# A third tile for the mixed rows, with its bytes taken from shared homes

## The chip, the cores and the metric

The kernel runs on one core of a Trainium2 chip. The metric is the device time of one execution in microseconds. The kernel before was run three times: 2610.47, 2618.05 and 2623.62 us, median 2618.05.

## The reference

Two residual layers act on x of shape (16, 16, 256, 256), batch and channel first. Cut to what is computed:

```python
def _L0_conv_ref(x, weight):          # 3x3 circular convolution, by way of FFTs
    ...
    return jnp.real(y).astype(x.dtype)

def _L1_conv_ref(x, ty, tx, weights_pole1, weights_pole2, weights_residue):
    alpha = jnp.fft.fft2(x, axes=(-2, -1))
    A = 1.0 / (omega1[:, None, None, None] - weights_pole1[None])
    Bm = 1.0 / (omega2[:, None, None, None] - weights_pole2[None])
    S = jnp.einsum('ikpq,oikp,xikq->oxik', weights_residue, A, Bm)
    output_residue1 = jnp.einsum('biox,oxik->bkox', alpha, S)
    C = jnp.einsum('biox,oikp->bikpx', alpha, A)
    D = jnp.einsum('bikpx,xikq->bikpq', C, Bm)
    output_residue2 = jnp.einsum('bikpq,ikpq->bkpq', D, weights_residue)
    x1 = jnp.fft.ifft2(output_residue1, s=(Ny, Nx), axes=(-2, -1)).real
    E1 = jnp.exp(weights_pole1[..., None] * tyc)
    E2 = jnp.exp(weights_pole2[..., None] * txc)
    F = jnp.einsum('kbpq,bipz->kbiqz', output_residue2, E1)
    x2 = jnp.einsum('kbiqz,biqx->kizx', F, E2).real
    return x1 + x2 / Nx / Ny

x = x + _L0_conv_ref(_gn(x), L0_conv_weight)
x = x + _L1_conv_ref(_gn(x), ...)
return x
```

`_gn` normalises groups of two channels. The second layer multiplies the spectrum of each image by a matrix S over channels that differs for every frequency (this is the mixing), transforms back, and adds a transient made of complex exponentials of the poles.

## The kernel before

The work runs in four stages, told apart in the trace by their matmuls.

1. From the start to about 565 us: the first layer's convolution (`ps_conv`, L305). Results go to DRAM (`vD`).
2. From 575 to 1194 us: the forward transforms. Spectra go to DRAM (`aD`), and the projections on the poles gather in `proj`.
3. Mixing, from about 1194 us: first `first_sums` and `finish_projections`, then, from 1219 to 1863 us, the loop that this text calls the mixing stage.
4. From 1860 us on: inverse transforms, the transient, and the output. It reads the mixed spectra `yD`, the exponentials `eD` and the projections `o2`.

**The mixing loop.** It goes over 32 groups g of frequencies, each in four steps n; a step is one pass of the loop body. In a step,

- `sums(n, ...)` makes with 16 small matmuls a part of the mixing matrices of the next group (`ps_s`, L1032), and `spread` brings them into the tile `sg`, half by ACT (L1049) and half by shuffles on DVE (L1052);
- `mix` makes four PSUM tiles `ps_mix` with 16 matmuls each (L1120), and each is copied into a quarter of the tile `yt` (L1233), two or three by ACT and the rest by DVE;
- `store` sends the filled `yt` to `yD` with four DMAs (L1134), and `load` fetches the spectra of the next group into `abd` (L1102 and L1107), four DMAs in the steps n = 1, 2, 3 and none in n = 0;
- in the first three steps of a group, `weights` prepares on DVE (`u`, `v`) and, in the third, on POOL (`w`, L930) the factors of a later group;
- `next(exps)` does one piece of the exponentials.

All these DMAs are issued by SP's queue in the order of the code. Each engine works off its own instructions in order, and that order is written out by hand (`manual_schedule`): what stands behind a waiting instruction on its engine waits too. `yt` comes from a pool of two buffers of 8 KB a partition, so the evictions of a step wait for the landing of the stores of two steps before.

**The exponentials** (`make_exps`) are generators whose pieces are put behind the steps. A pair of exponentials takes seven pieces: POOL multiplies the time axis by the imaginary parts (`s_th`, L1180), finds the number of turns (`s_rn`, L1181 to L1184) and subtracts them in three products (`s_tmp`, L1190, and L1191); POOL then adds the phase and clamps (L1194, L1195) while ACT makes the real exponentials (`s_ex`, L1198); two pieces later ACT takes the sine (L1201); then POOL multiplies the two (L1203) and folds the result into `s_ex` (L1205); and in the last piece SP stores `s_ex` to `eD` (L1210), with two DMAs for each of the first eight pairs and one for each of the other eight. Every tile of this pool has one buffer. The pieces are taken from the second group on, and the first four only load; between the eighth and the ninth pair lie four more pieces.

**Projections.** `first_sums` adds the two halves of `proj` into `accs` (L1062). `finish_projections` multiplies `accs` by the swap matrix `jmat` (four matmuls, L1090 and L1091) and copies the result to `o2` (L1092). In the kernel before, `proj`, `o2` and `jmat` have places of their own for the whole run, and `jmat` is loaded among the first constants (L158).

Two more things bear on the change. A tile called `between` of 1.5 KB only holds a place between two others. And pools of the mixing stage lie over places that the stage before has given up (`reuse_waits="tile"`): the first write to a tile waits for the last use of what lay there.

Of the kernel before, what the change touches and what calls it, by code (L numbers as in the profile page):

```python
# [9 lines left out]
FP = mybir.dt.float32  # L10
AF = mybir.ActivationFunctionType
ALU = mybir.AluOpType
# [4 lines left out]
B = 16  # L17
C = 16
N = 256
P = 128  # L20
PI = float(np.pi)
# [3 lines left out]
def conv_then_laplace_kernel(ctx: ExitStack, tc: tile.TileContext, a: dict, out: bass.AP):  # L25
# [15 lines left out]
    nc = tc.nc  # L41
    x = a["x"]

    cp = ctx.enter_context(tc.tile_pool(name="const", bufs=1))
# [9 lines left out]
    def const(name, shape):  # L54
        t = cp.tile(shape, FP, name=name, tag=name)
        later_loads.append((t, a[name]))
        return t
# [1 line left out]
    cols = const("cols", [P, 24])  # L59
    kmask = const("kmask", [P, C])  # L60
    fold2 = const("fold2", [P, 2, 64])
    o2 = cp.tile([P, B, 2, 16], FP, name="o2", tag="o2")
    proj = cp.tile([P, 2, B, 16, 2], FP, name="proj", tag="proj")
    jmat = cp.tile([P, 3, P], FP, name="jmat", tag="jmat")

    def pitched(name, rows, row, *split):

# [69 lines left out]
    def load_x(b, h):  # L137
        t = xp.tile([P, 18, N + 2], FP, name="xt", tag="xt")
        for i, j in zip(PARTS, PARTS[1:]):
            load_part(t, b, h, i, j)  # L140
        return t
# [13 lines left out]
    own = m16[:, 0:C:2]  # L155
    load_consts()
    halves[1] = [load_x(1, h) for h in range(2)]
    nc.sync.dma_start(out=jmat, in_=a["jmat"])  # L158
    ones = tp.tile([P, P], FP, name="ones", tag="ones")
    nc.vector.memset(ones, 1.0)  # L160
    tiny = wp.tile([P, 8], FP, name="tiny", tag="tiny")
# [557 lines left out]
    def pool(stage, name, bufs=1, **kw):  # L719
        return stage.enter_context(tc.tile_pool(name=name, bufs=bufs, reuse_waits="tile", **kw))  # L720
# [150 lines left out]
    p2 = ExitStack()  # L871
# [72 lines left out]
    for u in range(len(units) + 1):  # L944
# [27 lines left out]
        if last is not None:  # L972
            first_slots(b0, spec, *done)
            if b0 == B - 4:
                project(i, psd)
                (nc.sync if i + 1 < C else nc.scalar).dma_start(
                    out=aD[:, 2 * i : 2 * i + 2], in_=spec.rearrange("p r f b -> p r (f b)")
# [3 lines left out]
    ptab.close()  # L981


    yp = pool(p2, "yt", 2)
    g0 = pool(p2, "sg0")
    a0 = pool(p2, "abd0")
    wp = pool(p2, "w", 2)
    ep = pool(p2, "exps")
    up["u"] = pool(p2, "u")
    a1 = pool(p2, "abd2")  # L990
    zp = pool(p2, "between")
    tp = pool(p2, "ct")
    a2 = pool(p2, "abd3")
    g1 = pool(p2, "sg1")
# [10 lines left out]
        z.tile([P, 4, 4, 16, B], FP, name=f"abd{j}", tag=f"abd{j}") for j, z in ((2, a1), (3, a2))  # L1005
    ]

    zp.tile([P, 384], FP, name="between", tag="between")
    ct = tp.tile([P, 4, 8, N], FP, name="ct", tag="ct")
    nc.sync.dma_start(out=ct, in_=cD)  # L1010
    def next_step(steps, w):
# [42 lines left out]
    def first_sums():  # L1054

        nc.gpsimd.memset(pair, 0.0)
        wt, w128 = at_once(first_weights), at_once(weights(32))
        load(0, 1)  # L1060
        steps, w1 = weights(1), None
        nc.vector.tensor_tensor(accs, proj[:, :, :, :, 0], proj[:, :, :, :, 1], ALU.add)  # L1062
        sg = new_sg(0)
        other = up["u"].tile([P, 2, 2 * C], FP, name="other", tag="other")
        for h, w in enumerate((wt, w128)):
            for n in range(4):
                fy = slice(P * h, P * h + P)
                ps = sums(n, w)
                spread(
                    n,  # L1070
                    (sg[:, fy], [z[:, :, fy].rearrange("p q n -> p n q") for z in ps]),
                    (other[:, 1 - h], [z[:, :, P * (1 - h)] for z in ps]),
                )
                if 4 * h + n in (3, 4, 5):
                    w1 = next_step(steps, w1)
        for h in range(2):
            o, d = sg[:, P * h], other[:, h]
            nc.vector.tensor_tensor(d, d, o, ALU.subtract)
            nc.vector.scalar_tensor_tensor(o, d, fixrow, o, ALU.mult, ALU.add)
        for jq in range(2, 4):  # L1080
            nc.gpsimd.memset(abd[jq], 0.0)
            load(0, jq)
        return sg, w1

    def finish_projections():


        for ro in range(2):
            ps = pm.tile([P, B, 16], FP, name="ps_o", tag="ps_mix")
            nc.tensor.matmul(ps, lhsT=jmat[:, 0], rhs=accs[:, ro], start=True, stop=False)  # L1090
            nc.tensor.matmul(ps, lhsT=jmat[:, 2 - ro], rhs=accs[:, 1 - ro], start=False, stop=True)  # L1091
            nc.vector.tensor_copy(o2[:, :, ro], ps)  # L1092

    def load(g, jq, rows=range(4)):


        if jq == 0:
            return
        for s in rows:
            src = aD[4 * g + s].rearrange("r (c h n) -> r c h n", c=4, h=4)  # L1100
            if jq == 1:
                nc.sync.dma_start(  # L1102
                    out=pair[s::4, s].rearrange("r c h j b -> r c (h j b)"),
                    in_=src[:, :, 0:2].rearrange("r c h n -> r c (h n)"),
                )
            else:
                nc.sync.dma_start(  # L1107
                    out=abd[jq][s::4, s].rearrange("r c j b -> r c (j b)"), in_=src[:, :, jq]
                )
# [51 lines left out]
    def make_exps(which):  # L1161


        pl = ep.tile([P, C, 2], FP, name="s_pl", tag="s_pl")
        nc.sync.dma_start(out=pl, in_=a[f"pole_e{which + 1}"])
        t = ep.tile([P, N], FP, name="s_t", tag="s_t")
        nc.sync.dma_start(out=t, in_=a[("ty", "tx")[which]].to_broadcast([P, N]))
        sign, phase, turns = (cols[:, 2 + 3 * which + j : 3 + 3 * which + j] for j in range(3))
        pim = ep.tile([P, C], FP, name="s_pim", tag="s_pim")
        for _ in range(4):  # L1170
            yield
        nc.gpsimd.tensor_scalar(pim, pl[:, :, 1], sign, None, ALU.mult)
        for q in range(8):
            th = ep.tile([P, 2, N], FP, name="s_th", tag="s_th")
            rn = ep.tile([P, 2, N], FP, name="s_rn", tag="s_rn")
            tmp = ep.tile([P, 2, N], FP, name="s_tmp", tag="s_tmp")
            ex = ep.tile([P, 2, N], FP, name="s_ex", tag="s_ex")
            for j in range(2):
                i = 2 * q + j
                nc.gpsimd.tensor_scalar(th[:, j], t, pim[:, i : i + 1], None, ALU.mult)  # L1180
            nc.gpsimd.tensor_scalar(rn, th, 1.0 / (2 * PI), turns, ALU.mult, ALU.add)  # L1181
            magic = 1.5 * 2.0**23
            nc.gpsimd.tensor_scalar(rn, rn, magic, None, ALU.add)
            nc.gpsimd.tensor_scalar(rn, rn, magic, None, ALU.subtract)  # L1184
            yield
            c1 = 6.28125
            c2 = float(np.float32(1.93500518798828125e-3))
            c3 = 2 * np.pi - c1 - c2
            for c in (c1, c2, c3):
                nc.gpsimd.tensor_scalar(tmp, rn, float(c), None, ALU.mult)  # L1190
                nc.gpsimd.tensor_tensor(th, th, tmp, ALU.subtract)  # L1191
                if c == c2:
                    yield
            nc.gpsimd.tensor_scalar(th, th, phase, 3.1415925, ALU.add, ALU.min)  # L1194
            nc.gpsimd.tensor_scalar(th, th, -3.1415925, None, ALU.max)  # L1195
            for j in range(2):
                i = 2 * q + j
                nc.scalar.activation(ex[:, j], t, AF.Exp, scale=pl[:, i, 0:1])  # L1198
            yield True
            yield  # L1200
            nc.scalar.activation(th, th, AF.Sin)  # L1201
            yield True
            nc.gpsimd.tensor_tensor(th, th, ex, ALU.mult)  # L1203
            for op, eo in ((ALU.add, 0), (ALU.subtract, 1)):
                nc.gpsimd.tensor_tensor(  # L1205
                    ex[:, :, eo * P : eo * P + P], th[:, :, 0:P], th[:, :, N - 1 : P - 1 : -1], op
                )
            yield
            for o in range(2 - which):
                nc.sync.dma_start(  # L1210
                    out=eD[which][o, :, 2 * q : 2 * q + 2].rearrange("p i e t -> p i (e t)"),
                    in_=ex,
                )
            yield

    p2.enter_context(tc.manual_schedule())
    accs = yp.tile([P, 2, B, 16], FP, name="accs", tag="yt")
    ahead, wt = first_sums()
    finish_projections()
    unmix = None  # L1220
    exps, late = chain(make_exps(0), make_exps(1)), None
    for g in range(32):
        sg, w_now = ahead, wt
        steps = weights(g + 2) if g < 30 else iter(())
        ahead = new_sg(g + 1) if g < 31 else None
        for n in range(4):
            evict = sums(n, w_now) if ahead is not None else []
            yt = yp.tile([P, 2, 4 * B, 16], FP, name="yt", tag="yt")
# [27 lines left out]
    ep = pool(p3, "et")  # L1256
# [353 lines left out]
```

## Time and profile before

| | us |
|---|---|
| median of three runs | 2618.05 |
| the profiled execution's own time | 2623.94 |
| its span, first to last instruction | 2622.1 |
| mixing stage, within the span | 1219 to 1863 |
| PE busy in the mixing stage | 604.0 |
| POOL busy in the mixing stage | 389.2 |

The page's first lines give each engine's share of the span, and a strip of 40 slices shows it over time:

```profile
PE 2468.6 (94%) x35314; PEld 1885.3 (72%) x35314; DVE 1980.8 (76%) x3772; ACT 1432.6 (55%) x2599; POOL 1290.5 (49%) x1179
...
PE   5998999989999999998999999999799999999998
...
POOL 1333378433333333333666645766555565555553
```

A digit is the busy share of a slice of 65.6 us in tenths. [...] The mixing stage fills the slices 19 to 29. In rows of the trace, "SPq" is SP's queue, whose rows are DMA issues and not transfers; `<-` in a wait names the one that ended it. Where two shapes are given, the first is that of the output, as partitions by elements. A name such as L1134 is line 1134 of the kernel before.

### The profile page before, as it was taken

How to read it: one execution, taken by the hardware profiler on the slowest of the kernel's cores; microseconds unless marked ns; L12 is line 12 of the kernel's file. 1: busy time of each engine (PE TensorE's matmuls, PEld its weight loads, DVE VectorE, ACT ScalarE, POOL GpSimd, SP SyncE). 2: the span in 40 equal slices, each digit the busy share in tenths (PEclk: the TensorE clock that was granted, in tenths of full speed). 3: DMA queues.
4: the chain of work that ended last, by engine and by line, in shares of the span. 5: the costliest groups of instructions: out<-in, count | busy, mean ns of one | idle time of the engine just before them, and what ended most of it. 6: DMA issues, size and time to landing. Idle time of an engine off the chain costs nothing.

```text
span 2622.1 us, 84262 instructions
## 1 busy us (share of the span) xinstructions
PE 2468.6 (94%) x35314; PEld 1885.3 (72%) x35314; DVE 1980.8 (76%) x3772; ACT 1432.6 (55%) x2599; POOL 1290.5 (49%) x1179
## 2 busy tenths in 40 slices
PE   5998999989999999998999999999799999999998
PEld 2444455567777777775878778788688888888887
DVE  7777788848888888887877878887276676667666
ACT  2565566666666666665666656666244444444443
POOL 1333378433333333333666645766555565555553
PEclk9999999989999999999999999999899999999999
DMA  7888878854655655655777777777988888888884
GB/s 274 276 279 282 294 270 294 297 211 177 240 195 209 242 220 194 245 225 190 225 229 214 226 225 222 222 227 228 253 302 289 291 292 279 299 289 287 291 287 174
DMA packets 318011, 653.17 MB, mean 249 GB/s; under 512 B 49174, under 2 KB 163990, under 8 KB 305728
## 3 DMA queue, kind: packets, MB, share of 16 engines
q1 hardware_dynamic: 316464, 640.57, 72.4%
q8 instruction: 278, 4.55, 0.7%
q0 software_dynamic: 896, 3.02, 0.4%
q10 hardware_dynamic: 272, 4.19, 0.4%
q14 instruction: 101, 0.83, 0.1%
HBM read 368.15 MB, written 280.36 MB: 247 GB/s over the span
## 4 chain that ended last, share of the span: by engine, by line
PE 58%; DVE 7%; DMA 4%; SPq 3%; ACT 3%; POOL 2%; issue 1%; ACTq 0%; DVEq 0%; POOLq 0%
PE ps_mix L1120 9%; PE ps_y L777 9%; PE ps_y L785 8%; PE ps_p L1361 7%; PE ps_f L1385 7%; PE ps_f L1386 7%; PE ps_x L820 5%; DMA yD<-yt 4%; PE ps_s L1032 2%; SPq L1134 2%; PE ps_h L1345 2%; PE psd L805 1%; DVE r L1394 1%; DVE ol L1396 1%; DVE ol L1397 1%
## 5 line engine op out<-in xcount | busy, mean ns | idle before, releaser
L1120 PE MATMUL ps_mix<-abd,sg 128*64 128x128 f32 x8192 | 482.2, 276 | 39.4 <-DMA yD<-yt 16.6
L1120 PEld LDWEIGHTS ps_mix<-abd,sg 128*64 128x64 f32 x8192 | 451.9, 138 | 92.9 <-ACT yt L1233 55.7
L1325 POOL TENSOR_TENSOR u<-yk 128x512 f32<-128x512 f32 (+1 forms) x268 | 358.2, 1369 | 314.7 <-PE ps_p L1361 249.1
L305 PE MATMUL ps_conv<-xt,wc 32*32 32x512 f32 x12288 | 445.6, 602 | 36.0 <-issue 26.1
L305 PEld LDWEIGHTS ps_conv<-xt,wc 32*32 32x32 f32 x12288 | 251.1, 103 | 217.6 <-issue 127.0
L793 ACT ACTIVATE t<-ps_y,vmr 128x384 f32<-128x384 f32 x512 | 297.1, 580 | 161.1 <-PE ps_y L785 161.1
L1052 DVE STREAM_SHUFFLE sg<-ps_s 128x512 f32<-128x512 f32 (+1 forms) x264 | 329.1, 1316 | 0.0
L777 PE MATMUL ps_y<-tabE,vq 128*128 128x256 f32 x1024 | 313.2, 388 | 11.0 <-DVE vq L766 9.4
L785 PE MATMUL ps_y<-tabO,vq 128*128 128x256 f32 x1024 | 305.9, 380 | 0.0
L275 POOL TENSOR_TENSOR pair<-pair,far 128x1024 f32<-128x1024 f32 x64 | 151.7, 2370 | 304.1 <-DVE pair L272 207.7
L1385 PE MATMUL ps_f<-pt,inv 128*128 128x256 f32 x1008 | 300.4, 380 | 0.0
L1386 PE MATMUL ps_f<-hs,ey 128*128 128x256 f32 x1008 | 299.8, 379 | 0.0
L1361 PEld LDWEIGHTS ps_p<-inv,u 128*128 128x128 f32 x2048 | 268.9, 193 | 35.4 <-POOL u L1329 10.9
L1389 DVE TENSOR_TENSOR r<-ps_f,q 128x256 f32<-128x256 f32 x256 | 107.0, 418 | 241.9 <-ACT q L1388 241.9
L1361 PE MATMUL ps_p<-inv,u 128*128 128x128 f32 x2048 | 276.2, 278 | 9.8 <-POOL u L1329 9.7
L1049 ACT ACTIVATE sg<-ps_s,mcol 128x512 f32<-128x512 f32 (+1 forms) x264 | 179.3, 689 | 192.2 <-DVE sg L1052 117.1
L777 PEld LDWEIGHTS ps_y<-tabE,vq 128*128 128x128 f32 x1024 | 189.6, 191 | 87.5 <-ACT q L833 51.2
L1388 ACT COPY q<-ps_f 128x256 f32<-128x256 f32 x256 | 95.4, 373 | 274.7 <-PE ps_f L1386 250.4
L1363 ACT COPY pt<-ps_p 128x512 f32<-128x512 f32 x256 | 151.5, 592 | 134.9 <-PE ps_p L1361 134.9
L765 POOL TENSOR_TENSOR vq<-vf 128x512 f32<-128x512 f32 x64 | 81.4, 1272 | 291.6 <-DVE vf L769 281.5
L785 PEld LDWEIGHTS ps_y<-tabO,vq 128*128 128x128 f32 x1024 | 195.4, 191 | 26.9
L1233 ACT COPY yt<-ps_mix 128x512 f32<-128x512 f32 x352 | 184.1, 592 | 55.8 <-DMA yD<-yt 42.2
(237 smaller groups left out, 3993.6 us busy)
## 6 DMA issues: line engine op xcount, KB each, us to landing
xt<-in_x SPq DMA_DIRECT2D x288, 258.0 KB
vD<-pair SPq DMA_DIRECT2D x256, 256.0 KB
yD<-yt SPq DMA_DIRECT2D x512, 128.0 KB
vl<-vD SPq DMA_DIRECT2D x128, 512.0 KB
out_y<-ol SPq DMA_DIRECT2D x128, 512.0 KB
s<-vD SPq DMA_DIRECT2D x126, 512.0 KB
aD<-spec SPq DMA_DIRECT2D x15, 4096.0 KB
yk<-yD SPq DMA_DIRECT2D x60, 1024.0 KB
```

The lines of the kernel that those rows point to most:

```text
L305: nc.tensor.matmul(acc[r][32 * c : 32 * c + 32], lhsT=ready[b][0][rows, phase, tap], rhs=halves[b][u // 2][rows, q : q + 5 : 4, 2 - tap : ...
L777: nc.tensor.matmul(ps[:, 0:N], lhsT=vf[:, xo, 0, j], rhs=tabE[:, 0 : i + 2 : i + 1], start=True, stop=False, skip_group_check=True,)
L785: nc.tensor.matmul(ps[:, P : P + N], lhsT=vf[:, xo, 1, j], rhs=tabO[:, i : C + 1 : C - i], start=False, stop=True, skip_group_check=True,)
L793: nc.scalar.activation(t[:, xo, j].rearrange("p l n -> p (l n)"), ps[:, 0:384], AF.Copy, scale=vmr[:, 0, b0 + j, i : i + 1],)
L1049: nc.scalar.activation(to[..., k : k + 2], src[odd], AF.Copy, scale=nsgn)
L1052: nc.vector.stream_shuffle(to[..., C + k : C + k + 2], src[1 - odd], swap)
L1120: nc.tensor.matmul(ps[64 * t : 64 * t + 64, j], lhsT=sg[:, f : f + 2].rearrange("p f m -> p (f m)"), rhs=abd[jq][:, :, 2 * t + cc, 2 * jj ...
L1233: (nc.vector.tensor_copy if m >= (2 if late else 3) else nc.scalar.copy)(o, src)
L1325: nc.gpsimd.tensor_tensor(u[:, :, j].rearrange("p b (c n) -> p c b n", c=8), in0, in1, o)
L1361: nc.tensor.matmul(ps[:, at], lhsT=u[:, n], rhs=tab, start=True, stop=True)
L1385: nc.tensor.matmul(ps[:, e], lhsT=tab, rhs=pt[:, e], start=True, stop=False)
L1386: nc.tensor.matmul(ps[:, e], lhsT=ey[:, e], rhs=hs, start=False, stop=True)
```

## The change

The pool of `yt` gets a third buffer, 8192 bytes a partition more. They come from five places:

- `o2` (2048) is written into the place of `proj`, which is no longer needed once `accs` has been made;
- `jmat` (1536) is loaded at the start of the mixing, into the place of `s_ex`, which the exponentials use only later;
- `between` (1536) goes;
- `s_rn` has half its size (1024), and `s_tmp` goes (2048): the turns of the two exponentials of a pair are found and subtracted one after the other, and the products are written into `s_ex`, where ACT's real exponentials come to stand afterwards.

With that, the pieces of a pair are cut differently: the first is the two products for `s_th` and all nine instructions of the first half, the second the nine of the second half; the third begins with phase and clamp. There are seven pieces as before. The number of SP's DMAs doesn't change.

```diff
--- before.py
+++ after.py
@@ -59,9 +59,7 @@
     cols = const("cols", [P, 24])
     kmask = const("kmask", [P, C])
     fold2 = const("fold2", [P, 2, 64])
-    o2 = cp.tile([P, B, 2, 16], FP, name="o2", tag="o2")
     proj = cp.tile([P, 2, B, 16, 2], FP, name="proj", tag="proj")
-    jmat = cp.tile([P, 3, P], FP, name="jmat", tag="jmat")
 
     def pitched(name, rows, row, *split):
 
@@ -155,7 +153,6 @@
     own = m16[:, 0:C:2]
     load_consts()
     halves[1] = [load_x(1, h) for h in range(2)]
-    nc.sync.dma_start(out=jmat, in_=a["jmat"])
     ones = tp.tile([P, P], FP, name="ones", tag="ones")
     nc.vector.memset(ones, 1.0)
     tiny = wp.tile([P, 8], FP, name="tiny", tag="tiny")
@@ -981,14 +978,13 @@
     ptab.close()
 
 
-    yp = pool(p2, "yt", 2)
+    yp = pool(p2, "yt", 3)
     g0 = pool(p2, "sg0")
     a0 = pool(p2, "abd0")
     wp = pool(p2, "w", 2)
     ep = pool(p2, "exps")
     up["u"] = pool(p2, "u")
     a1 = pool(p2, "abd2")
-    zp = pool(p2, "between")
     tp = pool(p2, "ct")
     a2 = pool(p2, "abd3")
     g1 = pool(p2, "sg1")
@@ -1005,7 +1001,6 @@
         z.tile([P, 4, 4, 16, B], FP, name=f"abd{j}", tag=f"abd{j}") for j, z in ((2, a1), (3, a2))
     ]
 
-    zp.tile([P, 384], FP, name="between", tag="between")
     ct = tp.tile([P, 4, 8, N], FP, name="ct", tag="ct")
     nc.sync.dma_start(out=ct, in_=cD)
     def next_step(steps, w):
@@ -1082,14 +1077,19 @@
             load(0, jq)
         return sg, w1
 
+    jmat = ep.tile([P, 3, P], FP, name="jmat", tag="s_ex")
+    nc.sync.dma_start(out=jmat, in_=a["jmat"])
+
     def finish_projections():
 
+        o2 = cp.tile([P, B, 2, 16], FP, name="o2", tag="proj")
 
         for ro in range(2):
             ps = pm.tile([P, B, 16], FP, name="ps_o", tag="ps_mix")
             nc.tensor.matmul(ps, lhsT=jmat[:, 0], rhs=accs[:, ro], start=True, stop=False)
             nc.tensor.matmul(ps, lhsT=jmat[:, 2 - ro], rhs=accs[:, 1 - ro], start=False, stop=True)
             nc.vector.tensor_copy(o2[:, :, ro], ps)
+        return o2
 
     def load(g, jq, rows=range(4)):
 
@@ -1172,25 +1172,24 @@
         nc.gpsimd.tensor_scalar(pim, pl[:, :, 1], sign, None, ALU.mult)
         for q in range(8):
             th = ep.tile([P, 2, N], FP, name="s_th", tag="s_th")
-            rn = ep.tile([P, 2, N], FP, name="s_rn", tag="s_rn")
-            tmp = ep.tile([P, 2, N], FP, name="s_tmp", tag="s_tmp")
+            rn = ep.tile([P, N], FP, name="s_rn", tag="s_rn")
             ex = ep.tile([P, 2, N], FP, name="s_ex", tag="s_ex")
             for j in range(2):
                 i = 2 * q + j
                 nc.gpsimd.tensor_scalar(th[:, j], t, pim[:, i : i + 1], None, ALU.mult)
-            nc.gpsimd.tensor_scalar(rn, th, 1.0 / (2 * PI), turns, ALU.mult, ALU.add)
             magic = 1.5 * 2.0**23
-            nc.gpsimd.tensor_scalar(rn, rn, magic, None, ALU.add)
-            nc.gpsimd.tensor_scalar(rn, rn, magic, None, ALU.subtract)
-            yield
             c1 = 6.28125
             c2 = float(np.float32(1.93500518798828125e-3))
             c3 = 2 * np.pi - c1 - c2
-            for c in (c1, c2, c3):
-                nc.gpsimd.tensor_scalar(tmp, rn, float(c), None, ALU.mult)
-                nc.gpsimd.tensor_tensor(th, th, tmp, ALU.subtract)
-                if c == c2:
-                    yield
+            for j in range(2):
+                z, tmp = th[:, j], ex[:, j]
+                nc.gpsimd.tensor_scalar(rn, z, 1.0 / (2 * PI), turns, ALU.mult, ALU.add)
+                nc.gpsimd.tensor_scalar(rn, rn, magic, None, ALU.add)
+                nc.gpsimd.tensor_scalar(rn, rn, magic, None, ALU.subtract)
+                for c in (c1, c2, c3):
+                    nc.gpsimd.tensor_scalar(tmp, rn, float(c), None, ALU.mult)
+                    nc.gpsimd.tensor_tensor(z, z, tmp, ALU.subtract)
+                yield
             nc.gpsimd.tensor_scalar(th, th, phase, 3.1415925, ALU.add, ALU.min)
             nc.gpsimd.tensor_scalar(th, th, -3.1415925, None, ALU.max)
             for j in range(2):
@@ -1216,7 +1215,7 @@
     p2.enter_context(tc.manual_schedule())
     accs = yp.tile([P, 2, B, 16], FP, name="accs", tag="yt")
     ahead, wt = first_sums()
-    finish_projections()
+    o2 = finish_projections()
     unmix = None
     exps, late = chain(make_exps(0), make_exps(1)), None
     for g in range(32):
```

## What it will do to the time

> **What bounds the kernel now.** I read the page first, then the waits, the chain and the timeline of the mixing stage alone (1219 to 1863 us of the span, from the first `ps_mix` matmul at 1219.12 to the end of the last store), because everything the change touches runs there.
>
> ```profile
> span 2622.1 us, 84262 instructions
> ...
> ACT yt L1233 <- DMA yD<-yt: 42.2, 28, 10.3
> DVE yt L1233 <- DMA yD<-yt: 17.0, 12, 3.5
> PE ps_mix L1120 <- DMA yD<-yt: 16.6, 12, 3.2
> ...
> 1577.14 3.64 PE ps_mix L1120 x64
> 1581.81 3.64 PE ps_mix L1120 x64
> 1586.48 3.64 PE ps_mix L1120 x64
> ```
>
> The waits (total us, times, longest) show the symptom that a third tile would treat: the evictions into `yt` wait until the store that last used that tile has landed. The three chain lines show PE unhindered: one step (64 mixing matmuls, 16 sums) each 4.67 us. The stage has 128 steps; 124 x 4.67 + 4 x 3.71 (no sums in the last group) = 594 us, and the first matmul to the end of the last takes 641. So PE loses 47 us, and the question is what sets the other pace. I looked at the queue that stores:
>
> ```profile
> 1404.83 1.25 SPq L1107 DMA_DIRECT2D abd<-aD  x2
> 1406.18 1.02 SPq L1210 DMA_DIRECT2D eD<-s_ex  x2
> 1407.31 3.32 SPq L1134 DMA_DIRECT2D yD<-yt  x4
> 1410.73 1.23 SPq L1102 DMA_DIRECT2D abd<-aD  x2
> 1412.07 2.24 SPq L1134 DMA_DIRECT2D yD<-yt  x4
> 1414.36 2.44 SPq L1102 DMA_DIRECT2D abd<-aD  x2
> 1416.91 2.15 SPq L1134 DMA_DIRECT2D yD<-yt  x4
> 1419.16 2.53 SPq L1107 DMA_DIRECT2D abd<-aD  x4
> 1421.80 2.48 SPq L1134 DMA_DIRECT2D yD<-yt  x3
> ```
>
> Each row is start, length, count. The end of one is the start of the next: SP issues without a pause. Added over the stage's timeline, its issues take 0.555 us per store and 0.71 per load on average, with 0.05 between; gaps over 0.12 us with a releaser, and semaphore waits over 0.1 us, come to only 10 us in all. A group of four steps has 16 stores and 12 loads: 16 x 0.605 + 12 x 0.76 = 18.8 us, with the exponentials' stores 19.3, against PE's 4 x 4.67 = 18.7 and a measured 19.9. So SP's issuing is the pace, and `yt` waits because SP is late: a deeper buffer lets the evictions run further ahead of the same queue.
>
> [...] the real waits stand as gaps (2.08 us before the load at 1389.69). [...] The trace has 1281 ns at 512 and 731 at 256: 2.15 ns per element and 0.18 us fixed; so twice as many half-size instructions cost more.
>
> **The change part by part.**
>
> *Third `yt` tile.* Removes most of the waits above. What it can give is bounded by SP's own 10 us of waiting, not by PE's 47. The clearest piece is at the end: ACT's longest wait, 10.3 us, is in the last group, where the third step's tile waits for the first step's store; with a third tile the last store's 3.7 us wait on SP goes. Gain 4 there and about 1 before the exponentials start: 5 us.
>
> *`o2` in the place of `proj`, `jmat` loaded later.* One issue moves from the first stage to just after `ct` on SP. SP issued `ct` at 1173.61 and then waited until 1209.20 for the loads of `abd`, and `jmat` is first read at 1216.17: 0.6 us of issue inside 35 us of waiting, and about 5 us to land. If its place in SBUF were released late it would hold back the `abd` loads, needed at 1219, landing 4 us after issue; the places under it are the previous stage's, whose ACT and PE work ends by 1195. Cost nothing, at most 2 us. `o2` is written by DVE after DVE has read `proj`. Three small loads (`p2k`, `kgrp`, `mcol`) move early, and four ACT copies (`w`, 1.7 us) move behind two others, where DVE's shuffles begin only at 1203: nothing.
>
> *Scratch of the exponentials.* This is the expensive part. Per pair of exponentials (16 pairs):
>
> ```profile
> L1190 POOL TENSOR_SCALAR s_tmp<-s_rn 128x512 f32<-128x512 f32 x48 | 71.6, 1491 | 4.1
> L1191 POOL TENSOR_TENSOR s_th<-s_th,s_tmp 128x512 f32<-128x512 f32 x48 | 61.5, 1281 | 4.0
> L1180 POOL TENSOR_SCALAR s_th<-s_t,s_pim 128x256 f32<-128x256 f32 x32 | 29.3, 926 | 0.8
> ...
> L1205 POOL TENSOR_TENSOR s_ex<-s_th 128x256 f32<-128x256 f32 x32 | 22.7, 731 | 1.3
> L1181 POOL TENSOR_SCALAR s_rn<-s_th,cols 128x512 f32<-128x512 f32 x16 | 11.1, 693 | 1.7
> ...
> 1416.00 0.91 ACT L1198 ACTIVATE s_ex<-s_t,s_pl 128x256 f32<-128x256 f32 x2
> 1416.81 1.28 ACT L1049 ACTIVATE sg<-ps_s,mcol 128x512 f32<-128x512 f32 x2
> 1418.15 1.07 ACT L1233 COPY yt<-ps_mix 128x512 f32<-128x512 f32 x2
> ```
>
> Nine POOL instructions of 512 become eighteen of 256; at 926 and 731 ns, and an estimated 0.45 for half of L1181, POOL gains about 3 us a pair. By itself free: POOL is busy 389 of 644 us, and its 178 us of waiting for `v` (L930) covers 48.
>
> But the products now go into `s_ex`. Before, POOL's scratch had a place of its own, so it ran while the store of the previous pair was still queued; `s_ex` was written by ACT's Exp. Now the first product must wait until the previous pair's `eD<-s_ex` stores have landed, and ACT's Exp into the same bytes must wait until POOL's last product of each half has been used: in the compiled changed program the first product waits for those DMAs, and both Exp wait for POOL (before, only the first, on work long done). Behind the Exp on ACT stand the next step's `sg` and its `yt` evictions (the last two lines), and behind those SP's stores. A loop closes: SP issues `eD` -> lands -> POOL -> Exp -> evictions -> SP.
>
> From the first issue of `eD` of a pair, averaged over the 14 pairs with a predecessor seven steps earlier (the ninth has eleven):
> - to landing: 3.9 us (by the updates of its semaphores: 2.7 to 5.5);
> - POOL: three products and subtractions of the first half, then all nine instructions of the second. With the gaps of the timeline (0.08 between dependent ones), 3 x (1.0 + 0.82) = 5.5 and 0.54 + 2.0 + 5.5 = 8.0: 13.4 us. If the scalar ones scale down to half of 1.49 it is 12.0; if half of L1181 is not cheaper, 13.7. I take 13.4, since 926 is measured at 256;
> - `w` (1.9 us) falls between the halves in one pair of four: 0.5;
> - second Exp: 0.5. Sum 18.3.
>
> Before, the Exp of these pairs began 8.5 to 12.1 us after that issue, mean 10.0, and ended at 10.9. ACT is late by 7.4 us. The next step's first store came on average 2.0 us after its eviction (SP's lateness), which absorbs that much: 5.4 us of SP standing still per pair. As a loop: 18.4 to the end of Exp with the semaphore, 3.1 to the end of the next evictions (as before), then 18.9 from that step's store to the next `eD` issue (mean of before; it is SP's issuing, 16 stores and 12 loads, so it stays): 40.4 us, where before seven steps took 35.1. Also 5.3. Three tiles don't help, since the order within ACT holds all evictions behind the Exp. 14 x 5.3 = 74 us.
>
> *Sum.* The profiled execution took 2623.94 (span 2622.1 and 1.8 around it): 2623.9 + 74 - 5 = 2693. It stands 5.9 above the median of the three shown, 2618.05; against the median I predict 2687.
>
> **Rivals.**
> - *The mixed tile was the bound.* All `yt` waits go and PE sets the pace: -47, about 2571. For it: the chain gives `DMA yD<-yt` 15% of the stage. Against: SP's track is solid. Decided by whether an issue gets shorter when nobody waits.
> - *The loop stays hidden, SP-bound as before* (not slower): it holds if the POOL work after landing takes under about 8 us, so that Exp ends by 10.9 + 2 us after the issue. Then only SP's waits go: -5 to -10, about 2610. Against it, 15 instructions on POOL cannot average 0.53 us when the cheapest is estimated at 0.45 and six at 0.73.
> - *Half a loop.* Landing at 3.4, POOL at 12.0, no `w` between: 2.9 us a pair, 41 in all: about 2653. A deeper lead of the evictions over SP would act the same way.
> - *More than the loop.* Landing 4.5, POOL 13.7, SP's round 20 us since it starts without backlog: 7.2 a pair, 101 in all: about 2715.
>
> **How the numbers follow.** Forecast 0.62, half a loop 0.15, more 0.11, hidden 0.07, mixed tile 0.05. Range 2640 to 2722: from the half loop less 10 to the larger one with 7 for what runs differ. A measurement of this kernel can tell about 0.5% (13 us) from no change. Faster 0.05, same 0.07, slower 0.88.
>
> **What would show it.** In the changed profile: a POOL wait ended by `eD<-s_ex` in front of the product, some 14 times; ACT's Exp waiting for POOL, 5 to 9 us each; SP gaps in front of L1134 after it; `DMA yD<-yt` waits nearly gone; two pairs' `eD` issues about 40 us apart instead of 35; the mixing stage at about 710 us. I am wrong if the Exp rows show no wait, if `eD` issues stay at 35 us, or if SP's issue rows get shorter.

## The result, and the profile after

| | before | after |
|---|---|---|
| median, us (6 runs each) | 2619.66 | 2716.98 |
| range | 2610.47 to 2624.27 | 2711.82 to 2722.15 |
| span of the profiled execution | 2622.1 | 2709.9 |
| first `ps_mix` matmul to the last issue of a `yD` store | 643.5 | 732.3 |
| PE busy from 1300 to 1800 us | 471.6 | 424.0 |

The ratio is 1.0373, 95% interval 1.0356 to 1.039: slower by 97 us in the medians, and by 88 between the two profiled executions. The mixing stage alone is 89 us longer, so the whole loss between the profiles is there. The line numbers of the changed kernel are a few lower: its first product is L1190, the subtraction L1191, Exp L1197, the `eD` store L1209, the evictions into `yt` L1232; L1120, L1134 and the loads keep theirs.

First the span from the page, then the waits of the changed kernel in its mixing stage, 1219 to 1950 us (total us, times, longest):

```profile
span 2709.9 us, 84372 instructions
...
ACT s_ex L1197 <- POOL s_th L1191: 113.2, 22, 8.8
DVE sg L1047 <- ACT sg L1044: 112.3, 21, 9.9
PEld ps_mix L1120 <- ACT yt L1232: 85.1, 40, 8.1
...
PE ps_mix L1120 <- ACT yt L1232: 67.8, 12, 7.6
POOL s_ex L1190 <- DMA eD<-s_ex: 57.1, 10, 8.9
...
PEld ps_s L1027 <- POOL w L927: 24.0, 7, 8.7
```

Read from the row of `POOL s_ex` upwards: POOL's first product waits for the landing of the previous pair's stores; ACT's Exp waits for POOL; TensorE and DVE wait for what stands on ACT behind the Exp. Neither of the first two waits is in the list of the kernel before. Of the rows `yt <- DMA yD<-yt`, 42 and 17 us before, 1.2 us is left: the waits that the third tile was aimed at are gone, and the time went up.

One turn of the loop, from the timeline of the changed kernel (start, length; what stands in brackets is the wait before it and who ended it):

```profile
1338.76 1.03 SPq L1209 DMA_DIRECT2D eD<-s_ex  x2
...
1344.92 0.85 POOL L1190 TENSOR_SCALAR s_ex<-s_rn 128x256 f32<-128x256 f32 x1
...
1350.13 0.51 ACT L1197 ACTIVATE s_ex<-s_t,s_pl 128x256 f32<-128x256 f32 x1 [2.15 <-POOL s_th L1191]
...
1357.08 0.72 POOL L1191 TENSOR_TENSOR s_th<-s_th,s_ex 128x256 f32<-128x256 f32 x1
1357.84 0.51 ACT L1197 ACTIVATE s_ex<-s_t,s_pl 128x256 f32<-128x256 f32 x1 [7.20 <-POOL s_th L1191]
...
1358.25 1.25 ACT L1044 ACTIVATE sg<-ps_s,mcol 128x512 f32<-128x512 f32 x2
...
1359.39 1.07 ACT L1232 COPY yt<-ps_mix 128x512 f32<-128x512 f32 x2
...
1360.03 6.37 PE L1120 MATMUL ps_mix<-abd,sg 128*64 128x128 f32 x64 [7.63 <-ACT yt L1232]
1361.43 1.77 SPq L1134 DMA_DIRECT2D yD<-yt  x4
```

The stores of `eD` are issued at 1338.76 and land at 1343.9. POOL comes to its first product a microsecond later, so in this turn it has no wait for the landing. It goes through both halves, and ACT's second Exp can't start before the last subtraction has read its product: 1357.84, 19 us after the issue. What stands behind the Exp on ACT follows at once, `sg` at 1358.25 and the evictions at 1359.39, and SP, whose last issue had ended at 1355.82, stands until 1361.43 for them. The averages over the 14 pairs that have a predecessor seven steps earlier, with the terms of the forecast:

| from the first `eD` issue of a pair, us | before | forecast | after |
|---|---|---|---|
| to the landing | 3.95 | 3.9 | 4.06 |
| to the end of the second Exp | 6.95 | 14.5 | 14.59 |
| to the end of the next step's evictions | 3.33 | 3.1 | 3.03 |
| to that step's first store | 1.99 | 0 | 0.06 |
| to the next pair's `eD` issue | 18.92 | 18.9 | 19.62 |
| sum | 35.15 | 40.4 | 41.37 |

(The landings are read from the updates of the DMAs' semaphores.) The 6.2 us that a turn grew make 87 us in 14 turns, of the 89 that the stage grew.

### The profile page after: what moved, and what is told of

It is laid out like the page before. It is cut to its first block, busy times and chain, and to the rows that moved or that the text cites. A ratio compares the mean times of both kernels' runs of the same rounds, so it can differ in the third digit from the quotient of the medians.

```text
span 2709.9 us, 84372 instructions
## 1 busy us (share of the span) xinstructions
PE 2494.6 (92%) x35314; PEld 1910.2 (70%) x35314; DVE 1973.5 (73%) x3772; ACT 1432.6 (53%) x2599; POOL 1321.8 (49%) x1323
## 4 chain that ended last, share of the span: by engine, by line
PE 59%; POOL 6%; DVE 6%; DMA 3%; SPq 2%; issue 1%; ACT 1%; ACTq 0%; DVEq 0%; POOLq 0%
PE ps_mix L1120 11%; PE ps_y L774 9%; PE ps_y L782 8%; PE ps_p L1360 7%; PE ps_f L1384 7%; PE ps_f L1385 7%; PE ps_x L817 4%; PE ps_s L1027 3%; POOL s_ex L1190 2%; POOL s_th L1191 2%; PE ps_h L1344 2%; PE psd L802 1%; DVE r L1393 1%; DVE ol L1395 1%; DVE ol L1396 1%
## 5 line engine op out<-in xcount | busy, mean ns | idle before, releaser
L1120 PE MATMUL ps_mix<-abd,sg 128*64 128x128 f32 x8192 | 503.2, 284 | 80.6 <-ACT yt L1232 67.8
L1120 PEld LDWEIGHTS ps_mix<-abd,sg 128*64 128x64 f32 x8192 | 472.8, 143 | 134.8 <-ACT yt L1232 85.1
L302 PE MATMUL ps_conv<-xt,wc 32*32 32x512 f32 x12288 | 444.2, 605 | 33.3 <-issue 23.8
L774 PE MATMUL ps_y<-tabE,vq 128*128 128x256 f32 x1024 | 313.4, 388 | 11.2 <-DVE vq L763 9.6
L1385 PEld LDWEIGHTS ps_f<-hs,ey 128*128 128x128 f32 x1008 | 191.5, 190 | 25.9
```

The costliest lines, as they stand in the source:

```text
L302: nc.tensor.matmul(acc[r][32 * c : 32 * c + 32], lhsT=ready[b][0][rows, phase, tap], rhs=halves[b][u // 2][rows, q : q + 5 : 4, 2 - tap : ...
L774: nc.tensor.matmul(ps[:, 0:N], lhsT=vf[:, xo, 0, j], rhs=tabE[:, 0 : i + 2 : i + 1], start=True, stop=False, skip_group_check=True,)
L1120: nc.tensor.matmul(ps[64 * t : 64 * t + 64, j], lhsT=sg[:, f : f + 2].rearrange("p f m -> p (f m)"), rhs=abd[jq][:, :, 2 * t + cc, 2 * jj ...
L1385: nc.tensor.matmul(ps[:, e], lhsT=ey[:, e], rhs=hs, start=False, stop=True)
```

## The experiments

The kernel before ran beside each of them; its medians there were 2622.16 us beside the first four kernels below, 2620.67 beside *two_yt_full*, *three_yt_own_even*, *before_act_loads* and *three_yt_even_act*, and 2620.43 beside the other four. What follows gives each kernel's difference from the median that belongs to it.

### The loop taken apart: two_yt_shared, two_yt_two_ex, two_yt_own, three_yt_own

*two_yt_shared* is the changed kernel with two mixed tiles.

```diff
-    yp = pool(p2, "yt", 3)
+    yp = pool(p2, "yt", 2)
```

> The changed kernel with two yt tiles in place of three; all else as changed. Theory loop (the products in s_ex close a loop SP - eD - POOL - Exp - evictions - SP): the third tile hardly matters while the loop sets the pace, so 2712 to 2728 us, eD issues of successive pairs again 40 to 42 us apart. Theory tile (the depth of yt matters by itself, and the shared scratch costs more than the measured difference): the stage loses what the third tile gave, up to 47 us: about 2760.

Measured: 2726.0 us, +103.8, ratio 1.0397 (1.0349 to 1.0446). The loss is there with two tiles as well, and the third tile seems to be worth some 7 us beside it (revised below). The waits `yt <- DMA yD<-yt` are 25 and 15 us in this kernel's stage, against 1.2 with three tiles.

*two_yt_two_ex* has two tiles too, and lets `s_ex` alternate between two places, so that the products no longer wait for the last pair's store. Exp still waits for POOL.

```diff
-            ex = ep.tile([P, 2, N], FP, name="s_ex", tag="s_ex")
+            ex = ep.tile([P, 2, N], FP, name="s_ex", tag=("s_ex", "s_ex2")[q % 2])
```

> The changed kernel with two yt tiles and with two places for s_ex, used by pairs in turn: the products no longer wait for the previous pair's store, but Exp still waits for the products. Theory loop, with the wait for the store as its main part: the loop is open, but Exp still comes behind POOL, whose products ended 1 to 6 us after Exp in the profile of before and now end 3 us later still; about 2 us of that is absorbed, so 2630 to 2680 us. If Exp's wait for POOL alone made the loss: 2700 to 2720. If the wait for the store alone did: 2614 to 2626.

Measured: 2679.26 us, +57.1, ratio 1.0217 (1.0173 to 1.026), at the upper edge of the first expectation. Taking the landing out of the loop gives back 47 us.

*two_yt_own* puts the products into the free half of the place of `proj` instead, with two tiles; *three_yt_own* does it with three.

```diff
-        o2 = cp.tile([P, B, 2, 16], FP, name="o2", tag="proj")
+        home = cp.tile([P, 2, B, 2, 16], FP, name="o2", tag="proj")
+        o2 = home[:, 0]
...
-                z, tmp = th[:, j], ex[:, j]
+                z, tmp = th[:, j], spare[:, j]
```

(`spare` is `home[:, 1]` seen as 128 x 2 x 256.)

> As three_yt_own with two yt tiles: what is left of the change is the half-size POOL work, the later jmat and o2 in the place of proj. Theory loop: these cost nothing, 2614 to 2626 us, the same as before. Theory POOL: 2690 to 2720.

> The changed kernel with three yt tiles, but the products go into the free second half of the place of proj (2 KB, of which o2 takes the first half) instead of into s_ex. Theory loop with SP as the pace behind it: the loop is open, only SP's own waits go: 2608 to 2618 us. Theory tile: PE sets the pace, 2571 to 2585. Theory POOL (the doubled number of POOL instructions costs, not the waits): still 2690 to 2720.

Measured: 2638.73 us with two tiles, +16.6, ratio 1.0076 (1.0049 to 1.0103), and 2633.32 with three, +11.2, ratio 1.0037 (1.0022 to 1.0053). That Exp stands behind POOL costs 57.1 - 16.6 = 40 us, and the two together are the loop. But both lie above what the loop theory allowed: 11 to 17 us of these kernels are not the loop. The waits of *two_yt_own* from 1219 to 1880 us name a candidate that the kernel before had at 0.9 us:

```profile
PEld ps_s L1027 <- POOL w L927: 23.3, 10, 3.1
...
PE ps_s L1027 <- POOL w L927: 20.9, 10, 2.8
```

### What the loop doesn't explain: two_yt_full, two_yt_full_pad, three_yt_own_even

*two_yt_full* goes back to the scratch of the kernel before and to two tiles, and keeps only the moves of `jmat` and `o2`, without the padding `between`. A part of its difference from the changed kernel:

```diff
-    yp = pool(p2, "yt", 3)
+    yp = pool(p2, "yt", 2)
...
-            rn = ep.tile([P, N], FP, name="s_rn", tag="s_rn")
+            rn = ep.tile([P, 2, N], FP, name="s_rn", tag="s_rn")
+            tmp = ep.tile([P, 2, N], FP, name="s_tmp", tag="s_tmp")
...
+            nc.gpsimd.tensor_scalar(rn, th, 1.0 / (2 * PI), turns, ALU.mult, ALU.add)
...
```

> Two mixed tiles and the scratch of the kernel before (rn and products 128x512 in memory of their own, its cut of the pieces); only the moves of jmat and o2 of the change are kept, and the padding is gone. Theory 'pieces' (the 12 to 20 us that stay when the products have their own place come from the half-size scratch work, whose first piece of 11 instructions, about 8.3 us against 5.4 before, stands in front of w on POOL): 2612 to 2625, a ratio within 0.003 of 1 and the sums' waits for w back under 2 us. Rival 'moves' (the late jmat or the place of o2 costs something): 2630 to 2640, as with two mixed tiles and the products in their own place.

Measured: 2632.16 us, +11.5, ratio 1.0037 (1.0021 to 1.0052). The sums' wait for `w` is down to 1.1 us, and the time is 5 of the 17 us lower: the time lies in the range of the rival. Its stage is no longer than that of the kernel before (644.0 us from the first `ps_mix` matmul to the last `yD` issue, against 643.5); what is lost lies ahead of it. These are the waits of SP's queue from 1150 to 1240 us, in this kernel and in the one before, where the load of `ct` is L1005 and L1010 (the last of the `aD` stores is issued by ACT):

```profile
SPq L1005 <- PE ps_x L817: 31.2, 1, 31.2
SPq L1102 <- DMA aD<-spec: 23.9, 1, 23.9
```

```profile
SPq L1102 <- DMA aD<-spec: 35.0, 1, 35.0
...
SPq L1010 <- DMA aD<-spec: 11.0, 1, 11.0
```

Without the padding `between`, `ct` comes to lie on bytes that the forward transforms use to their end. Its load waits 31 us for a matmul, and starts 3.7 us ahead of the last `aD` store instead of 23.8; the first mix starts 29.8 us after that store instead of 21.7. *two_yt_full_pad* puts the padding back and changes nothing else:

```diff
+    zp = pool(p2, "between")
     tp = pool(p2, "ct")
...
+    zp.tile([P, 384], FP, name="between", tag="between")
     ct = tp.tile([P, 4, 8, N], FP, name="ct", tag="ct")
```

> The same as two_yt_full, with the padding of 1.5 KB (the tile between) put back ahead of ct. Theory 'layout' (without the padding and without a third tile ct lies on bytes that the stage before frees late: its load began 4 us ahead of the last aD store of that stage in the two-tile kernels, 24 us ahead in the kernel before, and the first mix 8 us later): the load of ct begins some 24 us ahead of that store again, the first mix some 21.6 us after it, and the time is within 0.3% of the kernel before, 2612 to 2626. Rival 'moves' (the late jmat or o2's place cost the 10 us): 2628 to 2636 as without the padding.

Measured: 2621.24 us, +0.8, ratio 1.0003 (0.9988 to 1.0019), and the first mix comes 21.7 us after the last `aD` store. So the moves of `jmat` and `o2` cost nothing, and the padding is worth 10.7 us to a kernel with two tiles. In the changed kernel the third tile shifts `ct` far enough by itself: its load starts 24.3 us ahead of the last `aD` store, as before. In all four kernels with two tiles and no padding the load starts only 3.7 us ahead of that store, and the first mix comes 29.7 to 31.4 us after it: they carry this cost, and the changed kernel doesn't.

That revises two readings. If the 10.7 us are the same in each of the four, the third tile's own share is not -7 us but 97.3 - (103.8 - 10.7) = +4 us in the changed kernel, and 11.2 - (16.6 - 10.7) = +5 with products in their own place: nothing that these intervals can tell from zero. And half-size scratch work comes to 16.6 - 11.5 = 5 us with two tiles, which the intervals of these two kernels (7 and 4 us each way) can't tell from zero either; for it speaks that the stage of two_yt_own is 9 us longer in the profile (653.2 against 644.0). With three tiles, the half-size work and the tile together cost the 11.2 of three_yt_own, and that is clear of zero.

*three_yt_own_even* is three_yt_own with POOL's pieces cut elsewhere, about 6.7, 5.8 and 7.2 us instead of 8.3, 7.3 and 4:

```diff
                     nc.gpsimd.tensor_tensor(z, z, tmp, ALU.subtract)
-                yield
+                    if (j, c) in ((0, c2), (1, c1)):
+                        yield
```

> Three mixed tiles, products in the free half of the projections' place, and the same half-size instructions, cut elsewhere: pieces of about 6.7, 5.8 and 7.2 us in place of 8.3, 7.3 and 4. Theory 'pieces by their cut' (w waits behind the longest first piece): the sums' waits for w fall from 54 us to under 25 and the time from 2633 to 2612 to 2625. Rival 'pieces by their sum' (POOL has 3 us more work a pair wherever it is cut): 2628 to 2640, w still 40 us or more.

Measured: 2629.82 us, +9.2, ratio 1.0031 (1.0017 to 1.0045). The rows for `w` (PEld and PE together) fell from 54 to 39 us and the difference by 2: by the medians the cut matters little, as the rival has it.

### Who sets the pace: before_act_loads, three_yt_even_act, before_more_issues, before_half_loads, three_yt_half_loads

The forecast's claim that a third tile can give little rests on SP's issuing being the pace. *before_act_loads* and *three_yt_even_act* let ACT's queue issue half of the loads, in the kernel before and in three_yt_own_even:

```diff
         for s in rows:
+            eng = nc.scalar if g and s >= 2 else nc.sync
...
-                nc.sync.dma_start(
+                eng.dma_start(
```

> The kernel before, with 6 of the 12 loads of a group of four steps (rows 2 and 3 of each) issued by ACT's queue. Theory 'SP is the pace' (the mixing stage moves at SP's 28 issues a group, 18.8 us, and TensorE at 18.7 would otherwise lose little): SP's part falls to some 14.5 us a group, ACT takes up to 4 us a group and has 7 idle; the waits for yD<-yt shrink and the stage loses 15 to 45 us: 2575 to 2605. Rival 'two tiles are the pace' (the stores' landing holds the tiles whoever issues the loads): 2610 to 2625. Rival 'ACT pays' (its issues delay the evictions): 2630 to 2660.

> Three mixed tiles, own place for the products, the even cut, and half the loads on ACT's queue. Theory 'SP is the pace': with SP relieved the third tile can give what TensorE's own pace allows, 594 of the stage's 641 us in the kernel before: 2565 to 2600, and below the kernel before with ACT's loads. Rival 'two tiles are the pace': 2605 to 2625, no better than the same kernel with all loads on SP. Rival 'ACT pays': 2630 to 2660.

Measured: 2631.76 us, +11.1, ratio 1.0035 (1.0021 to 1.005), and 2660.17, +39.5, ratio 1.0163 (1.0134 to 1.0191). The first of these times lies in the range of the rival 'ACT pays', the second at its upper end, and no gain came. Whether SP or the two tiles are the pace isn't decided by this, since SP wasn't relieved. SP's waits in before_act_loads from 1300 to 1500 us:

```profile
SPq L1135 <- DMA abd<-aD: 25.2, 23, 4.3
SPq L1103 <- DMA abd<-aD: 17.5, 7, 4.2
SPq L1108 <- DMA abd<-aD: 4.9, 5, 1.3
```

SP stands 48 of 200 us, in front of stores and loads, for the landing of loads. With one queue no such wait stands in the list for this stretch. So waits came with the second queue: over the stage SP's issues are 152 us shorter than in the kernel before (422 against 574), and its pauses between issues 158 us longer (227 against 69). Why a store waits for the landing of a load isn't shown. ACT pays too: its 181 issues take 128 us of its own time, and how much of the loss that is, no run separates.

*before_more_issues* adds to SP's queue two transfers of 32 bytes a group that nothing reads:

```diff
             store(g, n, yt)
+            if n % 2:
+                at = slice(8 * n, 8 * n + 8)
+                nc.sync.dma_start(out=between[0:1, at], in_=a["jmat"][0:1, 0, at])
```

> The kernel before with two transfers of 32 bytes more a group of four steps on SP's queue (a piece of jmat into the padding, after the stores of the second and fourth step; nothing reads it). Theory 'SP is the pace': 64 issues of 0.55 to 0.65 us are added one for one to the stage, 35 to 42 us: 2652 to 2664. Rival 'SP is hidden' (tiles, transfers or TensorE set the pace): 0 to 10 us, 2618 to 2632.

Measured: 2634.63 us, +14.2, ratio 1.006 (1.0039 to 1.0082): between the two expectations. I had priced these issues like stores; their row reads

```profile
L1239 SPq DMA_DIRECT2D between<-in_jmat x64: 249/307/938, 1235.1 to 1874.7; - x64
```

(least, median and greatest ns). Their mean is 0.337 us, with the 0.05 between issues 25 us for all 64, of which 14 came out as time. Issues that move next to nothing lengthen the kernel, so SP's queue is a bound; they don't do so one for one. SP has no more pauses than before (69 us in the stage of either kernel), but its other 928 issues take 562 us in this profile and 574 in that of the kernel before. Why they got shorter is open.

*before_half_loads* and *three_yt_half_loads* leave out the loads of rows 2 and 3 after the first group, in the kernel before and in three_yt_own_even:

```diff
         for s in rows:
+            if g and s >= 2:
+                continue
```

> The kernel before without the loads of rows 2 and 3 after the first group, so that these rows are mixed from the first group's data; 6 of 28 issues a group are gone from SP's queue and a fifth of the stage's transfers with them. Theory 'SP is the pace': SP's round falls to some 15 us, and TensorE's pace with the waits for two mixed tiles is left, 600 to 625 of 641 us: 2580 to 2605. Rival 'SP is hidden': 2612 to 2625.

> three_yt_own_even (three mixed tiles, products in their own place) without the loads of rows 2 and 3 after the first group, so that these rows are mixed from the first group's data. Theory 'SP is the pace, and so the third tile gives nothing': with SP relieved the third tile takes the waits for two tiles away, the stage comes to 590 to 605 us, 2565 to 2590, 10 us or more below before_half_loads. Rival 'POOL or TensorE is the pace of three tiles': 2605 to 2625, not below before_half_loads.

Measured: 2589.21 us, -31.2, ratio 0.9889 (0.9858 to 0.9921), and 2614.95, -5.5, ratio 0.9977 (0.9962 to 0.9992). The windows from 1300 to 1800 us of the kernel before, of before_half_loads and of three_yt_half_loads (width, busy us of PE, PEld, DVE, ACT, POOL with counts, granted clock, share of the DMA engines, GB/s):

```profile
1300.00:1800.00 500.00, 471.62 (x9571) 399.56 (x9571) 406.84 (x728) 324.81 (x541) 325.27 (x249) 0.99 0.77 224
```

```profile
1300.00:1800.00 500.00, 496.35 (x10202) 420.51 (x10208) 425.27 (x769) 343.73 (x576) 345.53 (x262) 1.00 0.66 182
```

```profile
1300.00:1800.00 500.00, 477.12 (x9740) 403.73 (x9744) 409.77 (x740) 327.67 (x550) 354.60 (x375) 0.99 0.63 174
```

With SP relieved, TensorE is busy 496 of 500 us, with two tiles. The third tile has nothing left to give there; the third tile and the half-size work together lose 26 us again. So the first expectation of three_yt_half_loads failed, and its rival, POOL or TensorE as the pace, holds the time. TensorE waits for `w` there, by this row of its waits from 1219 to 1850 us:

```profile
PEld ps_s L1027 <- POOL w L927: 24.8, 8, 3.4
```

Leaving loads out takes transfers away too (the DMA engines' share fell from 0.77 to 0.66), so this pair alone doesn't separate issuing from moving; the issues of 32 bytes do that, for a part. No version that computes everything beat the kernel before. The nearest is two_yt_full_pad, which is as fast and leaves 3.5 KB a partition free.

## Why the prediction was right, and where not

The forecast was 2687, within 2640 to 2722; 2716.98 is inside, on the slow side. The direction and the mechanism hold; the growth was forecast at 69 us and came to 97. On the profiled executions the forecast of 2693 stands against 2711.82, and two terms make the 19 us between them: the turns, 14 us short, and the third tile's gain of 5 us, which didn't come. The other 11 us are no matter of the mechanism: the forecast took off 5.9 us because the profiled execution before lay so far above its median, and the one after lies 5.2 below its own. The rival "More than the loop" named 2715 and was nearer. Of its three terms only SP's longer round came true (20 us, measured 19.6); its turn would have grown by 7.2 us where 6.2 were measured, so that its total fits so well is luck. Point by point:

- **The loop.** Shown: its wait for the store costs 47 us and Exp behind POOL 40, and without both the kernel comes to within 11 us of the one before. POOL, `w` and the second Exp were forecast at 14.5 us after the landing and took 14.59. That this is so exact is luck in part: POOL's products with `w` among them took 13.5 us and not 13.9, and the 0.6 us from the landing to the first product, most of it in four turns in which POOL came late, stood in no sum. SP stood 5.8 us before the next step's first store, forecast 5.4.
- **The size of a turn** was short by 1.0 us, 14 us in all. The term at fault is the last, "it is SP's issuing, 16 stores and 12 loads, so it stays": 19.62 for 18.92. It didn't stay, in two ways: SP's issues in this stretch got shorter, 16.1 us for 17.0, and its pauses longer, 3.6 for 1.9. About half of the added pause stands one step later: call the step whose evictions wait for the Exp C+1, then SP's gap before the stores of C+2 averages 0.87 us against 0.11 before, up to 2.75 in single turns. Most of the rest stands in front of loads (L1102) that wait for mixing matmuls. The turn quoted above shows where the gap before C+2 comes from. Its windows (clock and columns as above):

```profile
1350.00:1360.00 10.00, 2.39 (x58) 1.61 (x54) 1.26 (x3) 2.67 (x6) 9.02 (x11) 0.76 0.56 160
1360.00:1366.00 6.00, 5.97 (x60) 5.97 (x62) 5.08 (x10) 3.15 (x6) 1.49 (x1) 0.54 0.55 145
1366.00:1372.00 6.00, 6.00 (x136) 4.60 (x132) 5.01 (x9) 4.21 (x7) 4.23 (x4) 1.00 0.50 124
```

  TensorE idles 7.6 us, from 1352.39 to 1360.03, and its granted clock is 0.5 from 1355.27 to 1365.51, so the full clock came back 5.5 us after the work did. The 64 matmuls of the step take 6.37 us instead of 3.71, and the stores of that step start at 1367.20, 2.7 us after SP was ready. The clock was on no list of mine. In the changed kernel's stage it is 0.5 seventeen times, for 3.41, 6.83 or 10.24 us, against three times in the stage of the kernel before. Each of the seventeen begins within a pause of TensorE of 2.5 to 8.5 us or at most 1 us after it; the other pauses in this stage, the longest of 1.8 us, have none. Such steps are common now: 16 of the 128 steps take over 4.2 us on TensorE, where 3 did before. But that they lengthen the turn isn't shown. The seven turns with more than 0.7 us of pause before C+2 average 19.4 us in this term, the other seven 19.9. What makes the 0.7 us stays open.
- **"By itself free"** for POOL's half-size instructions doesn't hold: they and the third tile cost 11 us together, and alone, with two tiles, 5 by medians that can't tell it from zero. The cover named, 178 us of POOL's waiting for `v`, is the wrong kind: it lies ahead of `w`, for want of `w`'s inputs, while a longer piece in front of `w` makes `w` late. TensorE's sums waited 0.9 us for `w` before and 23 in two_yt_own.
- **Third tile, 5 us.** The forecast that it gives almost nothing was right, and even 5 was too much: 4 to 5 us the other way, not to be told from zero. Its waits disappeared without a gain. That SP and TensorE (19.3 and 18.7 us a group) lie so close that either holds the stage fits this; a kernel with the third tile and nothing else changed, which would show it, wasn't measured.
- **`jmat` and `o2`, nothing.** Right: +0.8 us. That dropping `between` costs nothing here is luck, for the forecast didn't look at it: the third tile takes over its service to `ct`, and without that tile it would have been 10.7 us.
- **What would show it.** POOL waited for `eD<-s_ex` 10 times and not 14; where POOL came late to its piece, the store had landed. The `eD` issues are 41.4 us apart (forecast about 40), and the stage is 732 us long (forecast 710). One of the three signs of being wrong came up in small: SP's issue rows did get shorter, 547 ns a store on average for 555 and 682 a load for 709, with medians nearly the same (444 for 448, and 603 both times). A store of a quarter of `yt` took anything from 302 to 2066 ns in the kernel before, so not all of an issue's length is a fixed price. The forecast counted the whole of each issue row as SP's work, with no waiting in it, and that goes further than these traces do.

The 97 us, split by the kernels as differences of medians in this order: moves 0.8, half-size work 5, Exp behind POOL 40, the store 47, third tile 4. The intervals make the moves uncertain by 4 us and the half-size work by 8; two_yt_two_ex and two_yt_shared, with four runs each, have intervals of 11 and 13 us each way, so the three terms after it are uncertain by 13 to 17.

## What to carry to other kernels

A scratch tile that shares its home with a tile that another engine fills and a queue stores brings waits on both (here 57 us of POOL for the store and 113 of ACT for POOL), and the waits can close into a loop if that queue is itself the pace: follow the chain from the store's issue round to the next issue before taking the bytes. A deeper buffer whose wait comes from a late queue removes the wait and not the time (here 25 and 15 us of waits fell to 1.2, with a share of the time that can't be told from zero). And before a padding tile is dropped, see whose bytes the tile behind it will lie on.

## What the runs showed of the hardware

- A DMA issue of 32 bytes to one partition held SP's queue for 0.337 us on average (64 of them, in before_more_issues), a store of a quarter of `yt` for 0.555 and a load for 0.71 (in the stage of the kernel before): issues have different prices, and a small one isn't free.
- In the changed kernel, after 7.6 us without work, TensorE's granted clock was 0.54 over the next 6 us, and a step of 64 matmuls took 6.37 us instead of 3.71: here TensorE paid more for a stall than the stall's own length, by 2.7 us.
